# A two-layer graph network on one core: where the block C22 of an adding outer product is formed, with a new order of steps and new places beside it

## The chip, the core and the metric

The kernel runs on one core of a Trainium2 chip. The metric is the device time of one execution in microseconds (us); the figure quoted for a kernel is the median of several executions. The engines are called by the profile's short names: PE is TensorE (PEld its weight loads), DVE is VectorE, ACT is ScalarE, POOL is GpSimd, and SP is the engine whose queue issues nearly all DMAs. Each engine works its own queue in order and waits on semaphores where another engine's result is needed.

## The reference, cut to what matters

There are 128 graphs of 128 nodes with 512 features, all in fp32. Two layers follow one another, each with a residual and a layer norm:

```python
# layer 0
agg = einsum('bij,bjf->bif', adj, x) / max(sum(adj, -1), 1e-6)
x = layernorm(x + relu(concat([x, agg], 2) @ W.T))
# layer 1
Xw = x @ Wv + bv;  sj = Xw @ aw[:512];  si = Xw @ aw[512:]
a = adj * exp(leaky_relu(sj[:, None, :] + si[:, :, None] + ab, 0.2))
T = a / (sum(a, -1) + 1e-12)
H = x@Wk[0] + bk[0] + (T@x)@Wk[1] + bk[1] + (T@T@x)@Wk[2] + bk[2]
out = layernorm(x + relu(H))
```

## The kernel before, in words

**Groups and layers.** The graphs are worked in NG = 32 groups of G = 4. Layer 0 of all groups comes first, then layer 1 of all groups; the x between them goes through DRAM. Both layers multiply each group's transposed x with a weight matrix, and both do it by a Strassen-like scheme of seven block products in two levels. The change concerns layer 1. There the weights are `wg[o]`, o = 1 to 7, the outer level; each outer product is again made of seven products of 128x128 by 128x385.

**One outer product (`outer`, L613).** It is a generator of seven steps, named below O3.1 to O3.7 for outer product 3. It owns a *lane* of four PSUM banks called X, Y, W, Z. The lane `bA` is lane 1 and serves O1, O5, O7 and the combine; `bB` is lane 0 and serves O2, O6, O4, O3. Step by step: 1, a product into X, and ACT copies X to Y (L624); 2, a product into Z, and ACT copies Z to the SBUF tile s5 (L630; O5 adds a bias on DVE instead, L628); 3, a product onto X, and DVE writes W = X + s5 (L633); 4, a product onto Y, and Y is evicted as block C11; 5, a product onto X, and `direct` writes block C22 = X + s5 to SBUF (DVE, L657 or L670); 6, a product onto W, and W is evicted; 7, a product onto X, and X is evicted late, that is at the end of the step. The lane is then passed on with its banks turned: the next product's X is this one's Y, its Y this one's Z, its W this one's X, its Z this one's W.

**Two kinds.** O1 and O5 are *copying* (L652): evictions are ACT copies (L654). O2, O6, O7, O4, O3 are *adding* (L660): their result is added onto a block tile that another outer product left (`src`), so evictions are DVE additions (L663). For C22 the function `early` (L665) has POOL add the source block onto s5 in SBUF at step 3 (L667), and `direct` at step 5 has DVE add X and that s5 (L670). O3 adds onto the tile r after `sum_r` (POOL, L700) has added s to it.

**The combine (`combine`, L786), c.1 to c.8.** It multiplies the transition matrix TT twice: `one(b)` for b = 0 to 3 is a product of 512 columns, two DVE additions to v1 (L802, L803) and an ACT copy of the row back into the bank (L804); `two(b)` accumulates TT times v1 on top and DVE adds the residual late (L376). The order is one 0, one 1, one 2, two 0, one 3, two 1, two 2, two 3.

**What sets the order.** PE's order is written out by hand as lists of steps: PT (L829) for the passage from layer 0 to layer 1, PG (L830) for group 0 of layer 1, PB (L833) for groups 1 to 30, PL (L836) for group 31 with both its own O and c steps and a second combine x.1 to x.8 at the end. In PB, `o3.7` and `c.k` belong to the group before. One PB cycle has 57 steps: 49 products and 8 combine steps. Everything else is hung beside the steps: `PLACES_B` (L912) gives, for each other operation, a position of two per step counted from the start of the group's cycle (114 positions in a cycle): an even position 2s is run after the body of step s and before its late evictions, an odd one after them. `PLACES_M` and `PLACES_L` (L922, L927) do the same for the last two groups, `PLACES_S` for the passage. So the order of the list and the positions fix each engine's queue.

**The operations beside the steps** that the text speaks of: `x_turn` (DVE transpose of a loaded x tile, L255), `x_inner`, `x_s1` to `x_s4` (POOL sums of left blocks), `sum_r`, `sum_c` (POOL), `t_scores` (four small ACT operations, a DVE transpose L728, a DMA), `t_load`, `t_exp` (ACT, L750, L752), `t_sums` (POOL multiply L757, DVE reduce L759, a small ACT operation L760, DVE reciprocal L762), `t_norm` (ACT, and a DMA to DRAM), `t_back`, `t_turn` (DVE, L784), and for the layer norm `ln_mean`, `ln_scales` (POOL), `ln_var` (ACT, L500), `ln_apply` (ACT, L513), `y_store`; `load_left`, `load_y`, `load_adj` are SP's loads. For the last group `t_scores` builds a diagonal dg on DVE (L724), `t_exp` multiplies it with ones on PE, and `t_norm` turns the result with four PE products by the identity, each copied back by ACT (L777).

Of the kernel before, what the change touches and what calls it, by code (L numbers as in the profile page):

```python
# [16 lines left out]
def kernel(  # L17
# [15 lines left out]
    P = 128  # L33
# [62 lines left out]

    def load_adj(n):
        g = n % NG
        adjs[n] = p1.tile([P, G, N], FP, name="ag")
        nc.sync.dma_start(adjs[n], adj[g * G : (g + 1) * G].rearrange("b i j -> i b j"))  # L100

# [193 lines left out]
    def part(t, b, w=FH):  # L295
        return t[:, b[0], b[1], :w]
# [316 lines left out]
    def outer(lane, g, o, evict_y, direct, bias=False, early=None):  # L613
        need(*[("wg_load", o, i) for i in range(4)])
        n = NG + g
        X, Y, W, Z = [t[:, :BW] for t in lane]

        def prod(dst, k, start=False):
            mm(dst, left_of(n, o)[:, LEFT[k]], wg[o][:, RIGHT[k]], start)
        s5 = halves()[:, :BW]  # L620
        if bias:
            L_.copy(X, beta[:, 0])
        prod(X, 1, not bias)
        L_.copy(Y, X)  # L624
# [8 lines left out]
        V.tensor_add(W, X, s5)  # L633
        if early:
            early(s5)
        yield
        prod(Y, 2)
        evict_y(BY, Y)
        yield
        prod(X, 7)  # L640
        direct(X, s5)
        yield
        prod(W, 3)
        evict_y(BWW, W)
        yield
        prod(X, 4)
        late.append((evict_y, BX, X))
        a, b, c, d = lane
        lane[:] = [b, d, a, c]
        yield  # L650
# [9 lines left out]
    def adding(lane, g, o, dst, src, made=None):  # L660
        def evict(b, t):
            need(*[(made, g, {BY: 4, BWW: 6, BX: 7}[b])] if made else [])
            V.tensor_add(part(dst, b, BW), t, part(src, b, BW))  # L663

        def early(s5):  # L665
            need(*[(made, g, 5)] if made else [])
            S_.tensor_add(s5, s5, part(src, BZ, BW))  # L667

        def direct(X, s5):
            V.tensor_add(part(dst, BZ, BW), X, s5)  # L670
        yield from outer(lane, g, o, evict, direct, early=early)

    def o1(lane, g):
# [41 lines left out]
    def t_scores(g):  # L715
        need(("O3", g, 7), ("sum_c", g, 0), ("sum_c", g, 1))
        si = small.tile([P, G], FP, name="si")
        for p, t in ((0, rs[NG + g]), (1, last22[g])):
            L_.copy(sj[:, 2 * p : 2 * p + 2], t[:, :, 1, 381])
            L_.activation(si[:, 2 * p : 2 * p + 2], t[:, :, 1, 382], AF.Identity, bias=cc)  # L720
        if g == NG - 1:
            dg = p1.tile([P, G, N], FP, name="dg", tag="sb")
            for b in range(G):
                V.tensor_scalar(dg[:, b], ident, sj[:, b : b + 1], None, ALU.mult)  # L724
            Ts[g] = dg, si
            return
        turned = small.tile([P, R], FP, name="turned")
        V.transpose(turned, sj)  # L728
        d = dram.tile([R, Q, R], FP, name="scd")
        nc.sync.dma_start(d.rearrange("b q r -> q b r"), turned)  # L730
        Ts[g] = d, si

    def t_load(g):
        need(("t_scores", g))
# [4 lines left out]
        Ts[g] = T, si  # L739

    def t_exp(g):
        need(("t_load", g) if g < NG - 1 else ("t_scores", g))
        T, si = Ts[g]
        if g == NG - 1:
            dg, T = T, p1.tile([P, G, N], FP, name="T", tag="aT")
            pt = lanes[0][0]
            mm(pt, ones[:].to_broadcast([P, P]), dg, True)
        for b in range(G):
            src = T[:, b] if g < NG - 1 else pt[:, b * N : (b + 1) * N]
            L_.activation(T[:, b], src, AF.Prelu, bias=si[:, b : b + 1], alpha=SLOPE)  # L750
        Ts[g] = T, si
        L_.activation(T, T, AF.Exp)  # L752

    def t_sums(g):
# [10 lines left out]
    def t_norm(g):  # L765
        need(("t_sums", g))
        T, rr = Ts[g]
        for b in range(G):
            L_.activation(T[:, b], T[:, b], AF.Copy, scale=rr[:, b : b + 1])
        if g < NG - 1:  # L770
            swap_out(NG + g, T)
            return
        TTs[g] = p1.tile([P, G, N], FP, name="TT")
        for b in range(G):
            pt = lanes[0][1 + b // 2]
            mm(pt[:, b % 2 * N : (b % 2 + 1) * N], T[:, b], ident, b % 2 == 0)
            L_.copy(TTs[g][:, b], pt[:, b % 2 * N : (b % 2 + 1) * N])  # L777

    def t_back(g):
        Ts[g] = swap_in(NG + g)  # L780
# [5 lines left out]
    def combine(lane, g):  # L786
# [9 lines left out]
        v1 = {}  # L796

        def one(b):
            need(("O4" if b > 1 else "O3", g, 7), ("sum_c", g, 0), ("sum_c", g, 1))
            mm(at_[b], TTs[g][:, b], row(b, 0, F, 0), True)  # L800
            v = v1[b] = v1s[(g * G + b) % 3]
# [22 lines left out]
    def step(lane, name, g, k):  # L824
# [5 lines left out]
    PG = ("O5.1 O5.2 O5.3 O5.4 O2.5 O2.6 O6.1 O6.2 O5.5 O5.6 O5.7 O7.1 O6.3 O6.4 O7.2 "  # L830
          "O6.5 O2.7 O7.3 O6.6 O7.4 O6.7 O4.1 O4.2 O7.5 O4.3 O7.6 O7.7 O4.4 c.1 O4.5 "
          "O4.6 c.2 c.3 c.4 O4.7 O3.1 O3.2 O3.3 O3.4 c.5 c.6 c.7 c.8 O3.5 O3.6").split()
    PB = ("O1.1 o3.7 O1.2 O1.3 O2.1 O2.2 O1.4 O1.5 O1.6 O1.7 O2.3 O2.4 O5.1 O5.2 O5.3 O2.5 O2.6 O5.4 O5.5 "  # L833
          "O2.7 O6.1 O5.6 O6.2 O5.7 O7.1 O6.3 O7.2 O6.4 O6.5 O7.3 O6.6 O6.7 O7.4 O4.1 O4.2 O7.5 O4.3 O7.6 "
          "O4.4 O7.7 O4.5 c.1 c.2 O4.6 O4.7 O3.1 O3.2 c.3 c.4 O3.3 c.5 O3.4 c.6 c.7 c.8 O3.5 O3.6").split()
    PL = ("o3.7 O1.1 O1.2 O2.1 O1.3 O2.2 O1.4 O1.5 O1.6 O1.7 O2.3 O2.4 O5.1 O2.5 O2.6 O5.2 O2.7 O5.3 O5.4 O6.1 O5.5 O5.6 "  # L836
          "O6.2 O5.7 O6.3 O7.1 O6.4 O6.5 O7.2 O7.3 O7.4 O6.6 O7.5 O6.7 O7.6 O7.7 O3.1 O3.2 O3.3 O3.4 c.1 c.2 c.3 c.4 "
          "O3.5 c.5 c.6 c.7 c.8 O4.1 O3.6 O4.2 O3.7 O4.3 O4.4 O4.5 O4.6 O4.7 x.1 x.2 x.3 x.4 x.5 x.6 x.7 x.8").split()
    for s in PF:
        step(2 + "ABCD".index(s[0]), "F" + s[0], 0, int(s[2]))  # L840
    base = {}
# [39 lines left out]
    def place_op(n, pos, name, m, *a):  # L881
# [3 lines left out]
        else:  # L885
# [24 lines left out]
        ("load_adj", 1): 37, ("y_store", 0, 0): 161, ("ln_apply", 0, 0): 138, ("load_left", 2, 0): 78,  # L910
    }
    PLACES_B = {  # L912
        ("y_store", 0, 1): 281, ("sum_r", 0, 0): 80, ("sum_r", 0, 1): 84, ("sum_c", 0, 0): 115, ("ln_var", 0, 1): 229,
        ("x_inner", 1, 1): 34, ("load_y", 0, 0): 172, ("ln_var", 0, 3): 233, ("x_turn", 1, 0, 1): 29, ("t_turn", 0): 188,
        ("t_back", 0): 163, ("ln_var", 0, 2): 225, ("ln_mean", 0): 224, ("ln_apply", 0, 0): 245, ("x_s1", 1): 64,
        ("load_left", 2, 0): 83, ("y_store", 0, 0): 262, ("ln_apply", 0, 2): 274, ("load_left", 2, 1): 59,
        ("t_load", 0): 118, ("ln_var", 0, 0): 230, ("ln_apply", 0, 3): 255, ("x_turn", 1, 0, 0): 12, ("ln_scales", 0): 244,
        ("t_scores", 0): 117, ("t_norm", 0): 151, ("t_exp", 0): 139, ("load_y", 0, 1): 173, ("ln_apply", 0, 1): 255,
        ("x_s2", 1): 68, ("x_s4", 0): 49, ("x_turn", 1, 1, 0): 1, ("sum_c", 0, 1): 100, ("t_sums", 0): 150, ("x_s3", 1): 96,
        ("load_adj", 0): 116, ("x_inner", 1, 0): 36, ("x_turn", 1, 1, 1): 16,  # L920
    }
    PLACES_M = {  # L922
        ("ln_mean",): 213, ("ln_var", 1): 224, ("ln_scales",): 226, ("ln_var", 2): 222, ("ln_apply", 0): 234,
        ("ln_apply", 3): 237, ("ln_apply", 1): 230, ("y_store", 1): 255, ("ln_var", 0): 224, ("y_store", 0): 243,
        ("ln_var", 3): 213, ("ln_apply", 2): 242,
    }
    PLACES_L = {  # L927
        ("end_store", 2): 150, ("t_norm",): 115, ("sum_r", 0): 71, ("end_store", 0): 153, ("t_scores",): 105,
        ("sum_r", 1): 71, ("t_exp",): 107, ("end_apply", 0): 147, ("load_adj",): 96, ("end_apply", 1): 152,
        ("load_y", 1): 94, ("end_store", 1): 163, ("t_sums",): 111, ("end_stats", 3): 137, ("end_mean", 0): 125,  # L930
        ("end_apply", 2): 139, ("end_var", 1): 131, ("end_mean", 1): 130, ("end_stats", 2): 130, ("end_rstd", 2): 132,
        ("load_y", 0): 57, ("end_store", 3): 155, ("end_apply", 3): 151, ("end_scales",): 133, ("end_var", 0): 125,
        ("sum_c", 0): 76, ("end_rstd", 3): 145, ("sum_c", 1): 76,
    }
# [117 lines left out]
```

## Time and profile before

| what | value |
|---|---|
| median of three executions | 2092.91 us (2092.64 to 2092.97) |
| the profiled execution's own time | 2093.66 us |
| its span, first to last instruction | 2091.9 us |
| PE busy | 2074.7 us of the span |
| DVE, ACT, POOL busy | 1465.5, 1153.7, 1532.2 us |
| granted PE clock | 0.998 |
| layer 0 / passage and group 0 / groups 1 to 30 / rest | about 28 to 808 / 808 to 850 / 850 to 2027 / 2027 to 2092 us |

A row of a profile gives the engine, the line of the code, what is written and read by the program's names, how often, the time it was busy and the mean of one, and after the bar the idle time of the engine just before it with what ended that. In a timeline a row begins with its start and its duration in us, and the bracket at the end tells how long the engine stood idle before it and for whom. A fp32 product stands in the trace as two matmul records and two weight loads.

### The profile page before, as it was taken

How to read it: one execution, taken by the hardware profiler on the slowest of the kernel's cores; microseconds unless marked ns; L12 is line 12 of the kernel's file. 1: busy time of each engine (PE TensorE's matmuls, PEld its weight loads, DVE VectorE, ACT ScalarE, POOL GpSimd, SP SyncE). 2: the span in 40 equal slices, each digit the busy share in tenths (PEclk: the TensorE clock that was granted, in tenths of full speed). 3: DMA queues.
4: the chain of work that ended last, by engine and by line, in shares of the span. 5: the costliest groups of instructions: out<-in, count | busy, mean ns of one | idle time of the engine just before them, and what ended most of it. 6: DMA issues, size and time to landing. Idle time of an engine off the chain costs nothing.

```text
span 2091.9 us, 25884 instructions
## 1 busy us (share of the span) xinstructions
PE 2074.7 (99%) x7100; PEld 1330.3 (64%) x7100; DVE 1465.5 (70%) x3247; ACT 1153.7 (55%) x2883; POOL 1532.2 (73%) x1424
## 2 busy tenths in 40 slices
PE   9999999999999999999999999999999999999997
PEld 6778888888778886555555555555555555555553
DVE  6777777777777777666666666666666666666665
ACT  2656666666666666355455455455455455455454
POOL 5777888887767776867767767767767767767763
PEclk9999999999999999999999999999999999999999
DMA  9777766676667767335534434534534534534523
GB/s 207 171 189 194 180 178 178 161 190 194 158 165 190 188 171 237 87 86 122 115 87 122 115 86 122 115 86 122 115 86 124 114 86 124 113 87 122 115 66 116
DMA packets 429486, 287.13 MB, mean 137 GB/s; under 512 B 153497, under 2 KB 352281, under 8 KB 429340
## 3 DMA queue, kind: packets, MB, share of 16 engines
q1 hardware_dynamic: 428412, 284.15, 53.7%
q10 hardware_dynamic: 800, 1.31, 0.3%
q8 instruction: 56, 0.92, 0.2%
q14 instruction: 90, 0.74, 0.1%
q0 software_dynamic: 128, 0.01, 0.0%
HBM read 191.60 MB, written 93.79 MB: 136 GB/s over the span
## 4 chain that ended last, share of the span: by engine, by line
PE 96%; DMA 1%; POOL 1%; DVE 1%; ACT 0%; issue 0%; ACTq 0%; DVEq 0%; POOLq 0%
PE bA L151 50%; PE bB L151 45%; DMA big<-in_w0t_dram 1%; DMA yd<-y 0%; DMA xb<-in_x_dram 0%; DMA y<-in_x_dram 0%; PE bA L177 0%; POOL s L667 0%; POOL c L711 0%; POOL r L703 0%; ACT junk L500 0%; DVE y L376 0%; POOL xs L266 0%; POOL xs L270 0%; POOL xu L278 0%
## 5 line engine op out<-in xcount | busy, mean ns | idle before, releaser
L151 PE MATMUL bB<-big,xu 128*128 128x385 f32 (+1 forms) x1806 | 562.1, 434 | 0.7 <-DVE r L670 0.5
L151 PEld LDWEIGHTS bB<-big,xu 128*128 128x128 f32 x1806 | 341.8, 190 | 167.7 <-issue 44.8
L151 PE MATMUL bA<-big,xl 128*128 128x256 f32 (+1 forms) x1358 | 405.8, 416 | 0.4 <-DVE bA L471 0.3
L151 PE MATMUL bB<-big,xs 128*128 128x256 f32 (+1 forms) x1316 | 384.1, 416 | 0.0
L151 PEld LDWEIGHTS bA<-big,xl 128*128 128x128 f32 x1358 | 257.1, 190 | 100.1 <-issue 15.6
L151 PEld LDWEIGHTS bB<-big,xs 128*128 128x128 f32 x1316 | 249.1, 190 | 84.8 <-ACT bB L624 6.2
L151 PE MATMUL bA<-big,xu 128*128 128x256 f32 (+1 forms) x896 | 294.3, 440 | 0.4 <-DVE bA L633 0.2
L667 POOL TENSOR_TENSOR s<-s,r 128x385 f32<-128x385 f32 x128 | 128.1, 1001 | 182.2 <-DVE bB L633 139.1
L151 PE MATMUL bA<-c,TT 128*128 128x512 f32 x512 | 241.3, 593 | 0.0
L500 ACT ACTIVATE junk<-y,mv 128x512 bf16<-128x512 f32 x252 | 182.6, 725 | 89.5 <-POOL mv L495 85.3
L151 PEld LDWEIGHTS bA<-big,xu 128*128 128x128 f32 x896 | 162.0, 189 | 95.4 <-DVE r L657 19.3
L513 ACT ACTIVATE y<-y,mv,rstd 128x512 f32<-128x512 f32 x252 | 202.1, 815 | 0.6 <-POOL mv L508 0.6
L376 DVE SCALAR_TENSOR_TENSOR y<-bA,y 128x512 f32<-128x512 f32 x256 | 170.5, 684 | 23.4 <-PE bA L151 16.9
L151 PE MATMUL bA<-big,xs 128*128 128x385 f32 x448 | 173.7, 499 | 0.0
L151 PE MATMUL bB<-big,xl 128*128 128x385 f32 (+1 forms) x462 | 172.0, 480 | 0.8 <-ACT bA L452 0.4
L633 DVE TENSOR_TENSOR bB<-bB,s 128x385 f32<-128x385 f32 x128 | 72.5, 567 | 121.0 <-PE bB L151 83.2
L151 PEld LDWEIGHTS bA<-c,TT 128*128 128x128 f32 x512 | 97.2, 190 | 89.4 <-issue 48.8
L624 ACT COPY bB<-bB 128x385 f32<-128x385 f32 x128 | 60.1, 470 | 143.8 <-PE bB L151 143.8
L278 POOL TENSOR_TENSOR xu<-xu,xs 128x896 f32<-128x896 f32 x63 | 131.7, 2090 | 8.8 <-PE bB L151 8.8
L274 POOL TENSOR_TENSOR xl<-xu,xl 128x896 f32<-128x896 f32 x63 | 133.5, 2120 | 1.1
L270 POOL TENSOR_TENSOR xs<-xs,xu 128x896 f32<-128x896 f32 x63 | 132.0, 2095 | 2.4
L266 POOL TENSOR_TENSOR xs<-xl 128x896 f32<-128x896 f32 x63 | 131.3, 2085 | 0.0
(182 smaller groups left out, 3474.8 us busy)
## 6 DMA issues: line engine op xcount, KB each, us to landing
xb<-in_x_dram SPq DMA_DIRECT2D x256, 128.0 KB, 3.8
y<-in_x_dram SPq DMA_DIRECT2D x64, 512.0 KB, 4.2
yd<-y SPq DMA_DIRECT2D x64, 512.0 KB, 3.0
xb<-yd SPq DMA_DIRECT2D x256, 128.0 KB, 5.2
y<-yd SPq DMA_DIRECT2D x64, 512.0 KB, 4.6
out_dram<-y SPq DMA_DIRECT2D x62, 512.0 KB, 2.8
ag<-in_adj_dram SPq DMA_DIRECT2D x64, 256.0 KB, 5.1
sb<-sd SPq DMA_DIRECT2D x252, 64.0 KB, 3.2
```

The lines of the kernel that those rows point to most:

```text
L151: nc.tensor.matmul(dst, lhsT, rhs, start=start, stop=True, skip_group_check=True)
L266: S_.tensor_add(xs[n][:, 0], xl[n][:, 0], xl[n][:, 1])
L270: S_.tensor_sub(xs[n][:, 1], xs[n][:, 0], xu[n][:, 0])
L274: S_.tensor_sub(xl[n][:, 0], xu[n][:, 0], xl[n][:, 0])
L278: S_.tensor_sub(xu[n][:, 1], xu[n][:, 1], xs[n][:, 1])
L376: V.scalar_tensor_tensor(y, t, 0.0, y, ALU.max, ALU.add, accum_out=mvs[n][:, b, 0:1])
L500: L_.activation(junk, ys[n, b // 2][:, b % 2], AF.Square, bias=mvs[n][:, b, 0:1], accum_out=mvs[n][:, b, 1:2])
L513: L_.activation(y, y, AF.Identity, bias=mvs[n][:, b, 0:1], scale=rstds[n][:, b : b + 1])
L624: L_.copy(Y, X)
L633: V.tensor_add(W, X, s5)
L667: S_.tensor_add(s5, s5, part(src, BZ, BW))
```

## The change

In `adding`, the source block of C22 is no longer added onto s5 by POOL. DVE writes Z + source into the destination block, from the PSUM bank Z of step 2, and at step 5 adds X onto that destination block. For O6, O7, O4 and O3 this stands in step 3 behind W = X + s5; for O2 it stands in step 4 behind the eviction of Y. The lists PB and PL and the tables PLACES_B, PLACES_M and PLACES_L are replaced; PT, PG, PLACES_S and PLACES_A stay.

For the last group alone the transition matrix is made in another way. Its adjacency is loaded by blocks and turned by DVE (`adj_turn`). dg is built from si instead of sj; after the product with ones, ACT applies Prelu with bias sj and Exp pair by pair, so that the matrix comes out turned (`end_scores`). `end_rows` multiplies by the turned adjacency on DVE (two halves of 256 columns) and has PE sum over partitions by a product with ones; `end_norm` adds the epsilon, takes the reciprocal of 256 columns and multiplies, all on DVE. The four PE turns by the identity, their ACT copies, and `t_exp`, `t_sums`, `t_norm` are not run for that group.

Among the places moved in the PB cycle: `x_turn` (1,1,0) from position 1 to -5, which is step 54 of the cycle before; the other two-part turns to steps 7 and 9; `load_left` (2,1) from 59 to 70; `t_sums` to 149, in front of the late eviction of O2.7; `sum_r` (0,1) to 81 and (0,0) to 86; `load_adj` from 116 to 103, `y_store` (0,1) to 278, in front of `t_back` at 165.

```diff
@@ load_adj
+        if n == 2 * NG - 1:
+            adjs[n] = p1.tile([P, G, Q, R], FP, name="agb", tag="ag")
+            load_blocks(adjs[n], adj[g * G : (g + 1) * G])
+            return
@@ outer
         V.tensor_add(W, X, s5)
-        if early:
-            early(s5)
+        if early and o != 2:
+            early(Z)
         yield
         prod(Y, 2)
         evict_y(BY, Y)
+        if early and o == 2:
+            early(Z)
@@ adding
-        def early(s5):
+        def early(Z):
             need(*[(made, g, 5)] if made else [])
-            S_.tensor_add(s5, s5, part(src, BZ, BW))
+            V.tensor_add(part(dst, BZ, BW), Z, part(src, BZ, BW))

         def direct(X, s5):
-            V.tensor_add(part(dst, BZ, BW), X, s5)
+            V.tensor_add(part(dst, BZ, BW), X, part(dst, BZ, BW))
@@ new for the last group
+    def adj_turn():
+        need(("load_adj", 2 * NG - 1))
+        src = adjs[2 * NG - 1]
+        adjs[2 * NG - 1] = p1.tile([P, G, N], FP, name="agT", tag="aT")
+        V.transpose(adjs[2 * NG - 1].rearrange("p g n -> p (g n)"), src.rearrange("p g j r -> p (g j r)"))
+    def end_scores(g):
+        need(("t_scores", g), ("C", g - 1, 8))
+        (dg, _), pt = Ts[g], lanes[0][0]
+        mm(pt, ones[:].to_broadcast([P, P]), dg, True)
+        T = TTs[g] = p1.tile([P, G, N], FP, name="TT")
+        for b in range(G):
+            L_.activation(T[:, b], pt[:, b * N : (b + 1) * N], AF.Prelu, bias=sj[:, b : b + 1], alpha=SLOPE)
+            if b % 2:
+                L_.activation(T[:, b - 1 : b + 1], T[:, b - 1 : b + 1], AF.Exp)
+    def end_rows(g, h):
+        need(("end_scores", g), ("adj_turn",))
+        T = TTs[g][:, 2 * h : 2 * h + 2].rearrange("p b n -> p (b n)")
+        pt = lanes[0][1 + h][:, :FH]
+        V.tensor_mul(T, T, adjs[2 * NG - 1][:, 2 * h : 2 * h + 2].rearrange("p b n -> p (b n)"))
+        mm(pt, ones[:].to_broadcast([P, P]), T, True)
+    def end_norm(g, h):
+        need(("end_rows", g, h))
+        T = TTs[g][:, 2 * h : 2 * h + 2].rearrange("p b n -> p (b n)")
+        pt = lanes[0][1 + h][:, :FH]
+        rr = halves()[:, :FH]
+        V.tensor_scalar(rr, pt, ROW_EPS, None, ALU.add)
+        V.reciprocal(rr, rr)
+        V.tensor_mul(T, T, rr)
@@ order of steps, new lists
+    PB = ("O1.1 o3.7 O1.2 O1.3 O2.1 O1.4 O1.5 O1.6 O2.2 O1.7 O2.3 O2.4 O5.1 O5.2 O2.5 O5.3 O2.6 O5.4 O2.7 "
+          "O6.1 O5.5 O6.2 O5.6 O6.3 O5.7 O6.4 O7.1 O6.5 O6.6 O7.2 O7.3 O6.7 O4.1 O7.4 O7.5 O4.2 O4.3 O7.6 "
+          "O4.4 O4.5 O7.7 c.1 O4.6 O4.7 O3.1 O3.2 c.2 O3.3 c.3 c.4 c.5 c.6 c.7 c.8 O3.4 O3.5 O3.6").split()
+    PL = ("O1.1 o3.7 O1.2 O2.1 O1.3 O2.2 O1.4 O1.5 O1.6 O1.7 O2.3 O2.4 O5.1 O2.5 O5.2 O2.6 O2.7 O5.3 O5.4 O6.1 O5.5 O6.2 "
+          "O5.6 O5.7 O6.3 O7.1 O6.4 O6.5 O7.2 O7.3 O6.6 O7.4 O7.5 O6.7 O7.6 O7.7 O3.1 O3.2 O3.3 O3.4 c.1 c.2 c.3 c.4 "
+          "c.5 c.6 c.7 c.8 O4.1 O3.5 O4.2 O3.6 O3.7 O4.3 O4.4 O4.5 O4.6 O4.7 x.1 x.2 x.3 x.4 x.5 x.6 x.7 x.8").split()
@@ PLACES_B, new
+        ("t_norm", 0): 154, ("sum_r", 0, 1): 81, ("load_y", 0, 0): 170, ("ln_var", 0, 3): 230, ("x_turn", 1, 0, 1): 19,
+        ("t_back", 0): 165, ("x_s1", 1): 66, ("ln_scales", 0): 239, ("t_sums", 0): 149, ("x_turn", 1, 1, 1): 19,
+        ("load_left", 2, 0): 82, ("ln_var", 0, 1): 227, ("y_store", 0, 0): 264, ("t_turn", 0): 187, ("ln_var", 0, 2): 224,
+        ("sum_c", 0, 0): 109, ("ln_apply", 0, 2): 273, ("ln_apply", 0, 3): 257, ("x_inner", 1, 1): 53, ("ln_var", 0, 0): 235,
+        ("t_exp", 0): 140, ("load_left", 2, 1): 70, ("ln_apply", 0, 1): 257, ("y_store", 0, 1): 278, ("x_s2", 1): 68,
+        ("x_turn", 1, 1, 0): -5, ("x_s3", 1): 97, ("ln_apply", 0, 0): 242, ("t_load", 0): 123, ("t_scores", 0): 119,
+        ("x_turn", 1, 0, 0): 14, ("sum_r", 0, 0): 86, ("x_s4", 0): 42, ("load_adj", 0): 103, ("load_y", 0, 1): 190,
+        ("ln_mean", 0): 223, ("sum_c", 0, 1): 115, ("x_inner", 1, 0): 41,
@@ PLACES_L, new
...
+        ("end_store", 2): 158, ("sum_c", 1): 72, ("sum_r", 0): 71, ("end_store", 0): 158, ("t_scores",): 105,
+        ("end_var", 1): 134, ("sum_r", 1): 71, ("load_adj",): 96, ("load_y", 0): 47, ("end_apply", 1): 160,
+        ("load_y", 1): 106, ("end_mean", 1): 128, ("end_rows", 0): 111, ("end_mean", 0): 127, ("end_rstd", 2): 132,
...
+        ("sum_c", 0): 76, ("end_rstd", 3): 149, ("end_apply", 0): 144, ("end_scores",): 106, ("end_rows", 1): 111,
+        ("end_norm", 0): 111, ("end_stats", 3): 138, ("end_norm", 1): 111, ("end_apply", 3): 158, ("adj_turn",): 96,
```

## The prediction, made before the changed kernel was run

> **What bounds the kernel now.** I read first the busy shares, then busy time by stretch (us from the start; PE, PEld, DVE, ACT, POOL), then the weight loads' timeline in one steady cycle, then who held the weight loads between 860 and 2050, then DVE's timeline in group 0 and PE's at the end.
>
> ```profile
> PE 2074.7 (99%) x7100; PEld 1330.3 (64%) x7100; DVE 1465.5 (70%) x3247; ACT 1153.7 (55%) x2883; POOL 1532.2 (73%) x1424
> ```
> ```profile
> 850.50:2026.60 1176.10, 1175.49 (x3416) 636.96 (x3417) 778.14 (x1619) 607.58 (x1488) 863.77 (x777) 1.00 0.44 107
> 2064.00:2091.90 27.90, 15.50 (x38) 6.82 (x36) 13.15 (x34) 15.42 (x39) 6.76 (x14) 0.85 0.20 75
> ```
> PE is the bound, and idle only at the end. But a record lasts until its drain: a 385-column record is shown as 487 ns, while two in a row start 323 ns apart (512 columns: 429). So waits of up to 0.16 us lie inside "busy", and I read starts. A PB cycle holds 98 records of 385 and 16 of 512 columns: 98 x 0.323 + 16 x 0.429 = 38.52 us. Measured from cycle to cycle: 39.22. So 0.70 us per cycle is lost, 30 x 0.70 = 21 us in all; more than that this change cannot win there.
>
> ```profile
> 1012.65 0.19 PEld L151 LDWEIGHTS bA<-big,xu 128*128 128x128 f32 x1
> 1013.46 0.30 PEld L151 LDWEIGHTS bA<-big,xu 128*128 128x128 f32 x2 [0.62 <-DVE r L657]
> 1013.90 1.16 PEld L151 LDWEIGHTS bB<-big,xu 128*128 128x128 f32 x4
> 1015.56 0.94 PEld L151 LDWEIGHTS bA<-big,xs 128*128 128x128 f32 x4 [0.51 <-issue]
> 1017.03 0.30 PEld L151 LDWEIGHTS bA<-big,xs 128*128 128x128 f32 x2 [0.53 <-ACT bA L624]
> ```
> ```profile
> PEld bA L151 <- DVE r L657: 18.6, 30, 0.6
> PEld bA L151 <- ACT bA L624: 15.7, 30, 0.5
> PEld bA L151 <- DVE bA L633: 11.8, 30, 0.4
> ```
> Thirty of each: one per cycle (the time is that of PEld's idling, its usual rest included; what PE loses is less). By starts, O1.7 loses 0.27 us (O1.5 stands only two steps ahead and `direct` isn't done), O5.3 0.18 (the copy Y = X of O5.1, two steps ahead), O5.1 0.16 (ACT reaches the beta copy L622 late), O1.5 0.05 (its W). Sum 0.65; the rest is jitter. **None of the four waits for POOL**: `early` on POOL is hidden in the steady cycle. It costs only in group 0:
>
> ```profile
> 843.64 0.56 DVE L670 TENSOR_TENSOR c<-bB,s 128x385 f32<-128x385 f32 x1 [0.41 <-POOL s L667]
> 850.18 0.56 DVE L670 TENSOR_TENSOR r<-bB,s 128x385 f32<-128x385 f32 x1 [1.52 <-POOL s L667]
> ```
> ```profile
> 2066.00 1.12 PE L151 MATMUL bB<-dg,ones 128*128 128x512 f32 x2 [0.79 <-DVE dg L724]
> 2066.97 3.09 PE L151 MATMUL bA<-big,xl 128*128 128x385 f32 x8
> 2072.29 0.49 PE L151 MATMUL bB<-ident,T 128*128 128x128 f32 x2 [2.23 <-ACT T L769]
> 2073.32 1.14 PE L151 MATMUL bB<-ident,T 128*128 128x128 f32 x4 [0.54 <-ACT TT L777]
> ```
> The last fence is the end: PE waits for the last transition matrix, and the last combine starts at 2075.41.
>
> **The Trainium skill.** "Perfetto Trace Analysis", Identifying the Most-Contended Engine, says that matmul busy share is no measure because matmuls are pipelined: agrees (0.70 us per cycle hidden at 99%). "TensorE: Matmul & The Clock Gate", Specifications: PE pulls weight loads ahead of running matmuls. Agrees: undisturbed, a load starts 2 ns after the matmul before it; a waiting one isn't pulled, and starts 0.053 after the release, with 0.107 more before its product runs. **So PE stalls unless the reader has ended 0.16 us before** (0.22 where it waits for two engines). "GPSIMD Engine Reference", Specifications: no PSUM access, which is why `early` needed s5; no run here tests it.
>
> **The change, part by part.** I walk a cycle from T = 0 at O1.1, a product 0.646, a combine step 0.858. A reader of a product's bank starts 0.847 after the step's start (1.058 for a combine step); DVE then takes 0.56 (385 columns; next one starts 0.46 later), a turn 0.70 (0.625), ACT 0.47 (0.36 to 0.41), all from rows and starts around 1007 to 1046.
>
> *`early` on DVE.* Five POOL additions of 1.00 go per cycle, five DVE ones come: 2.3 (by spacing) to 2.8 us. DVE rises from 25.96 to some 28.5 of 39.2, POOL falls from 28.84 to 23.8. Queued behind each are the eviction of step 4 and `direct`. The work that covers it: W is written ahead of it, and PE needs `direct` only at step 7, at least three steps after step 5 in the new list wherever an adding product is concerned: 1.94 against 0.847 + 0.56 + 0.16 = 1.57. Without that cover it would cost up to 0.46 per product, 2.3 per cycle. I take 0.
>
> *New order.* O2.2 now stands between O1.6 and O1.7, O2.5 between O5.2 and O5.3: three steps each, 1.94 against 1.57 and 1.48. **Those 0.27 + 0.18 = 0.45 go.** What is late next:
> - c.5 to c.8 now run without a product between. c.5's additions, row copy and release: 1.058 + 0.343 + 0.412 + 0.089 + 0.592 + 0.16 = 2.654 against 3 x 0.858 = 2.574: 0.08. Before, in the last group, the same four in a row lost 0.10.
> - `x_turn` (1,1,0), moved to step 54, stands in DVE's queue ahead of `direct` of O3.5 and the eviction of O3.6. c.8's residual frees DVE at 37.48, eviction 37.48, turn 37.96, `direct` 38.59 to 39.14, + 0.16 = 39.30; o3.7 is due at 38.52 + 0.65 = 39.16: 0.14.
> - O1.5: s5 of O1.2, then `t_scores` on ACT, its DVE turn (L728), then W: 2.66 after O1.2 against 2.58: 0.08.
> - O5.1: eviction of O1.6, then `ln_apply`, s5 of O2.2, eviction, beta: 3.39 against 3.23: 0.16 as before.
>
> Sum 0.46 for 0.65: **0.19 to 0.20 per cycle, 29 cycles, 5.7 us.** Each of the four is good to about 0.1 either way.
>
> *Other places.* `t_sums` now stands ahead of O2.7's eviction and `direct` of O5.5. The chain (T's load issued at 5.2 lands 3.2 later, median of its issues; Prelu 9.1, Exp to 11.1, POOL multiply to 12.4, reduce to 13.2, reciprocal 13.6) frees `direct` at 14.0; O5.7 needs it by 15.5: cost 0, margin 0.96. SP: `y_store` stands ahead of `t_back`, which waits for its own swap anyway (sd lands 2.3 after 15.1); `load_left` (2,1) has 19 steps, 12.3 us, for four issues of 0.5 and 5.2 of landing; `load_adj`, now at the cycle's end, finds its buffer freed by the multiply at 12.4: 0. POOL queue: `sum_r` (0,1) comes before (0,0) and ends near 29.5, before O3's `early` at 32.1. ACT: in the last group one `ln_var` now stands ahead of `t_scores`; it ends at 2065.3 on the old clock, before r's block is there at 2065.5: 0.
>
> *Passage and group 0* (order unchanged). O4.7 waited 0.59 for L670 behind POOL; now only the two-step distance, 0.33: -0.26. o3.7 waited 0.80: gone. `sum_c` then ends 0.9 + 0.9 us earlier on POOL (two `early` less ahead), so O1.5's 0.46 shrinks to 0.04. Against it DVE is jammed from 822 to 828 by late residuals, and O2's `early` adds 0.45. Sum -1.0; bounds -1.6 to 0.
>
> *Last group.* o3.7 loses its 0.34. O3's `early` waits on DVE for `sum_r` half 1, queued second on POOL (done at 2055.15 by the old times): the eviction, then c.1's additions come behind it and c.4 loses 1.0. So dg's product starts 1.2 later, 2067.2. Then Prelu and Exp of the first pair to 2069.5, multiply, rows; Exp of the second to 2070.5, multiply, rows at 2071.0; add 0.40, reciprocal, multiply. **The reciprocal of 256 columns is in no row.** Low: 0.42, as a multiply of 256. High: the skill's "VectorE: DVE Perf Modes", First, the fixed hardware budget, gives it a repeat count of 8: an estimate of (256 x 8 + 151)/0.96 = 2.3 us. Its row of 4 elements takes 178 ns against 161 for an addition of 4: 4 ns more an element, so some 5.3 x 256 + 157 = 1.5 us. I take 1.5. Then x.1 starts at 2073.6 instead of 2075.4, but the second half's norm and O4.6's eviction behind it hold x.3 for 1.1 and x.4 for 0.9, where before the waits in the combine came to 1.05: PE ends 0.7 earlier, with o3.7 1.1. Bounds: -3.2 with 0.42, +0.6 with 2.3. The chain of norms and stores after it keeps its length.
>
> **Sum.** -5.7 - 1.0 - 1.1 = -7.8. The profiled execution took 2093.66 (span 2091.9 and 1.8 around it): 2085.9. The median shown is 0.75 lower, 2092.91: **2085.0.**
>
> **Rivals.**
> - *Clean*: all of 0.65 goes and no new wait comes (my 0.16 rule too strict): 2092.9 - 29 x 0.65 - 2.1 = 2072. For it: three of the new stalls are within 0.14 of nothing. Against: O5.1's chain is not touched.
> - *Moved*: the waits only change place, 0.6 to 0.7 per cycle: 2092.9 - 2.1 = 2091. For it: four margins below 0.1 that sum against me if ACT or DVE runs 0.05 later.
> - *Slower*: DVE's head. `t_sums`' reduce waits for POOL and ACT with `direct` of O5.5 behind it. It decides once T's chain is over 0.96 us later than walked; each us beyond costs PE one in every cycle. Half a us: 29 x 0.5 - 7.8, +6.7: 2100. For it: this wait is new at that place. Against: POOL's multiply is first in its queue now.
> - *Not done as said*: excluded; the edit is plain.
>
> **Numbers.** Forecast (2080 to 2089 by itself) 0.60, clean 0.13, moved 0.17, slower 0.10. A measurement tells 0.2%, 4.2 us, from no change. Faster: forecast nearly whole, clean: 0.72; same: moved and a rest: 0.18; slower 0.10. Range 2073 to 2092: it leaves out slower (0.10) and the far half of clean (0.06), and holds the bounds of passage and end (-4.8 to +0.6 for -2.1) and four stalls each 0.1 off with the same sign (29 x 0.4 = 12, taken halfway).
>
> **What would show it.** Cycle 39.02 by starts (38.6 clean, over 39.2 moved); no wait of PE on L657 at O1.7, nor on L624 at O5.3; waits at o3.7, O1.5, O5.1, c.8 of the sizes above; no L667; a reciprocal row of 256 columns near 1.5 us; x.1 near 2066.6 (2075.4 - 1.8 - 0.3 - 5.7 - 1.0). Wrong if the weight loads wait 30 times on a step not named here.

## The result, and the profile after

| | before | after |
|---|---|---|
| median, us (lowest to highest, runs) | 2092.91 (2092.63 to 2093.38, 5) | 2084.6 (2083.08 to 2085.31, 5) |
| profiled execution, us (its span) | 2093.66 (2091.9) | 2083.08 (2081.3) |
| one steady cycle by starts, us | 39.220 | 38.912 |
| start of the last group to the start of PE's last record, us | 55.41 | 55.61 |

The ratio is 0.9958, with an interval of 0.9948 to 0.9969: 8.3 us less. The profiled execution of the changed kernel is the fastest of its five, that of before lies 0.75 above its median, so the two traces differ by 10.6.

The busy shares first. VectorE rises by 60 us and POOL falls by 155, while PE stays at 99%:

```profile
PE 2062.5 (99%) x7096; PEld 1329.9 (64%) x7096; DVE 1525.8 (73%) x3414; ACT 1155.7 (56%) x2875; POOL 1377.7 (66%) x1263
```

Who held the weight loads between 855 and 2040 (waited-for line: us in total, times, longest):

```profile
PEld bA L155 <- ACT bA L831: 19.3, 31, 0.7
PEld bB L155 <- DVE r L676: 13.7, 29, 0.8
PEld bA L155 <- DVE bA L637: 9.2, 29, 0.3
PEld bA L155 <- DVE r L663: 0.6, 1, 0.6
```

The wait of O1.7 for `direct` (L663 here, L657 before) has fallen from 30 to one, in the last group, whose own list still has O1.7 two steps behind O1.5 (it loses 0.27 us there); the wait of O5.3 for the copy Y = X is gone. New are 29 waits for L676, the `direct` of O3 (o3.7), and for L831, the row copy of a combine (c.8). The same stretch of one cycle as a timeline of weight loads (start, us, engine, line, what; in brackets the idle time and its cause):

```profile
1083.16 0.30 PEld L155 LDWEIGHTS bB<-big,xu 128*128 128x128 f32 x2 [0.46 <-DVE r L676]
...
1086.37 0.97 PEld L155 LDWEIGHTS bA<-big,xu 128*128 128x128 f32 x4 [0.32 <-DVE bA L637]
...
1088.77 1.16 PEld L155 LDWEIGHTS bB<-big,xu 128*128 128x128 f32 x4
1090.44 0.94 PEld L155 LDWEIGHTS bA<-big,xs 128*128 128x128 f32 x4 [0.51 <-issue]
```

These are o3.7, O1.5, the run of loads from O2.2 over O1.7 to O2.3, now without a wait, and O5.1. Idle time of PEld is not PE's loss; by starts of the matmuls PE loses per cycle 0.113 us at o3.7, 0.161 at O5.1, 0.075 at c.8 and nothing at O1.5, whose load waits but is done in time. Sum 0.35, where before it was 0.65 (O1.7 0.270, O5.3 0.176, O5.1 0.156, O1.5 0.051).

The last group on PE and on VectorE:

```profile
2046.53 1.13 PE L155 MATMUL bA<-big,TT 128*128 128x512 f32 x2 [0.80 <-ACT bA L831]
...
2055.83 1.12 PE L155 MATMUL bB<-dg,ones 128*128 128x512 f32 x2 [0.78 <-DVE dg L730]
...
2062.70 1.13 PE L155 MATMUL bA<-c,TT 128*128 128x512 f32 x2 [1.04 <-DVE TT L770]
2065.74 1.98 PE L155 MATMUL bA<-c,TT 128*128 128x512 f32 x4 [1.92 <-DVE c L669]
```
```profile
2044.11 0.56 DVE L673 TENSOR_TENSOR r<-bB,r 128x385 f32<-128x385 f32 x1 [0.94 <-POOL r L709]
...
2060.43 1.75 DVE L769 RECIPROCAL s<-s 128x256 f32<-128x256 f32 x1
...
2063.01 1.75 DVE L769 RECIPROCAL s<-s 128x256 f32<-128x256 f32 x1
...
2065.14 1.02 DVE L669 TENSOR_TENSOR c<-bA,c 128x385 f32<-128x385 f32 x2
```

c.4 stalls behind `early` of O3, which waits on VectorE for POOL's second sum; the reciprocal takes 1.75 us; x.1 starts 6.87 us after dg's product (9.40 before), but x.2 then stalls for 2.19 us: its bank is the W of O4, and O4.6's eviction of it stands on VectorE behind the second half's norm (it ends at 2065.69; x.2 starts at 2065.74).

Span by stretches, after against before: the start and the first layer, which the change leaves alone, 0.9 less; passage and group 0, 1.3 less; 29 cycles 8.9 less (the first 0.24 of o3.7's old wait in the last group is counted here); the last group 0.2 more, with 0.28 more behind PE's last record. Sum -10.6.

### The profile page after: what moved, and what is told of

It is laid out like the page before. It is cut to its first block, busy times and chain, and to the rows that moved or that the text cites. A ratio compares the mean times of both kernels' runs of the same rounds, so it can differ in the third digit from the quotient of the medians.

```text
span 2081.3 us, 25875 instructions
## 1 busy us (share of the span) xinstructions
PE 2062.5 (99%) x7096; PEld 1329.9 (64%) x7096; DVE 1525.8 (73%) x3414; ACT 1155.7 (56%) x2875; POOL 1377.7 (66%) x1263
## 4 chain that ended last, share of the span: by engine, by line
PE 97%; DVE 1%; DMA 1%; ACT 0%; issue 0%; POOL 0%; SPq 0%; ACTq 0%; DVEq 0%
PE bA L155 51%; PE bB L155 46%; DMA yd<-y 0%; DMA xb<-in_x_dram 0%; DMA y<-in_x_dram 0%; PE bA L181 0%; DVE s L769 0%; DVE y L380 0%; POOL r L709 0%; ACT y L517 0%; DVE big L995 0%; DVE xl L259 0%; DVE xu L259 0%; DVE big L1003 0%; SPq L83 0%
## 5 line engine op out<-in xcount | busy, mean ns | idle before, releaser
L155 PE MATMUL bB<-big,xu 128*128 128x385 f32 (+1 forms) x1806 | 569.5, 435 | 1.0 <-DVE c L676 0.7
L155 PE MATMUL bA<-big,xl 128*128 128x256 f32 (+1 forms) x1358 | 395.9, 416 | 0.3 <-DVE bA L475 0.3
L155 PE MATMUL bB<-big,xs 128*128 128x256 f32 (+1 forms) x1316 | 388.8, 416 | 0.0
L155 PEld LDWEIGHTS bA<-big,xl 128*128 128x128 f32 x1358 | 256.8, 189 | 100.1 <-issue 15.5
L155 PE MATMUL bA<-c,TT 128*128 128x512 f32 x512 | 245.9, 592 | 3.0 <-DVE c L669 1.9
L380 DVE SCALAR_TENSOR_TENSOR y<-bA,y 128x512 f32<-128x512 f32 x256 | 170.4, 683 | 19.6 <-PE bA L155 13.4
L155 PE MATMUL bA<-big,xs 128*128 128x385 f32 x448 | 178.3, 492 | 0.0
L709 POOL TENSOR_TENSOR r<-r,s 128x770 f32<-128x770 f32 x64 | 115.1, 1820 | 86.4 <-DVE c L669 86.4
L155 PE MATMUL bB<-big,xl 128*128 128x385 f32 (+1 forms) x462 | 167.2, 480 | 0.5 <-ACT bA L456 0.4
L790 POOL TENSOR_TENSOR T<-ag,T 128x512 f32<-128x512 f32 x31 | 39.5, 1275 | 175.9 <-ACT T L785 175.9
L499 POOL TENSOR_SCALAR mv<-mv 128x4 f32<-128x4 f32 x63 | 14.5, 230 | 212.3 <-DVE y L380 212.3
L831 ACT COPY bA<-r 128x512 f32<-128x512 f32 x64 | 37.7, 590 | 176.4 <-DVE big L830 170.7
L637 DVE TENSOR_TENSOR bB<-bB,s 128x385 f32<-128x385 f32 x128 | 72.5, 567 | 85.1 <-PE bB L155 75.4
```

The costliest lines, as they stand in the source:

```text
L155: nc.tensor.matmul(dst, lhsT, rhs, start=start, stop=True, skip_group_check=True)
L380: V.scalar_tensor_tensor(y, t, 0.0, y, ALU.max, ALU.add, accum_out=mvs[n][:, b, 0:1])
L499: S_.tensor_scalar(mvs[n][:, :, 0], mvs[n][:, :, 0], -1.0 / F, None, ALU.mult)
L709: S_.tensor_add(r, r, s)
L790: S_.tensor_mul(T, adjs[NG + g], T)
L831: L_.copy(at_[b], row(b, 254, 766, 1))
```

## The experiments

Each kernel was run beside the kernel before on the same chip; the last columns are the difference of the two medians and the steady cycle in its trace. The changed kernel stands at -8.3 in this table.

| kernel | us | before there | difference | cycle |
|---|---|---|---|---|
| 1 move alone | 2092.63 | 2092.77 | -0.1 | 39.204 |
| 2 all but the move | 2095.20 | 2092.77 | +2.4 | 39.286 |
| 3 turn later | 2081.32 | 2092.77 | -11.5 | 38.851 |
| 4 `ln_apply` later | 2079.38 | 2092.77 | -13.4 | 38.751 |
| 5 O3.4 between | 2099.45 | 2093.28 | +6.2 | 39.416 |
| 6 sums exchanged | 2085.92 | 2093.28 | -7.4 | 38.912 |
| 7 old last group | 2086.30 | 2093.28 | -7.0 | 38.912 |
| 8 exponentials later | 2096.44 | 2093.28 | +3.2 | 39.300 |
| 9 addition twice | 2098.24 | 2093.84 | +4.4 | 39.297 |
| 10 three waits mended | 2075.61 | 2093.84 | -18.2 | 38.641 |
| 11 and O3.4 between | 2086.47 | 2093.84 | -7.4 | 39.022 |

The theory: the gain is the order of steps, which takes two waits off PE; `early` on VectorE is hidden. The rival: POOL was the brake, and taking work off it gains. No run takes the new list and the new places apart for O1.7 and O5.3. That the list frees them is read from the traces: with three steps instead of two in between they lose nothing, and O1.7 of the last group, still at two, loses its 0.27.

**1. The move alone**, in the kernel before (the calls of `early` are changed with it, and O2's stands in step 4, as in the change):

```diff
-            S_.tensor_add(s5, s5, part(src, BZ, BW))
+            V.tensor_add(part(dst, BZ, BW), Z, part(src, BZ, BW))
...
-            V.tensor_add(part(dst, BZ, BW), X, s5)
+            V.tensor_add(part(dst, BZ, BW), X, part(dst, BZ, BW))
```

> The kernel before with only the fifth product's addition moved to VectorE; step order, places and end as before. Theory (the order is the gain, the move by itself is hidden): the four waits of a steady cycle (O1.7, O5.3, O5.1, O1.5) wait for nothing on POOL, so the cycle stays at 39.22 us; group 0 and the passage gain about 1.3, the last group loses about 0.6 because O3's addition now holds VectorE until POOL has summed half 1 of r: 2092.2 us. Rival (the move off POOL is what gains): the whole change of about 8 us is here, cycle 38.9, 2084.5 us.

Ratio 0.9998 (0.999 to 1.0007): nothing. The four waits stand as before (O1.7 0.269, O5.3 0.175, O5.1 0.154, O1.5 0.040). Passage and group 0 give 1.15 back, and in the last group c.4 loses 1.06. The rival "POOL was the brake" falls for the old order.

**2. All but the move**: the changed kernel with the four lines of 1 turned round (O2's addition, on POOL again, stays in step 4).

> The changed kernel with the fifth product's addition back on POOL; order, places and new end kept. Plain form of the theory (order alone): cycle stays 38.91, passage +1.3, last group -1.0, 2085 us. Refined form, from POOL's queue walked with the five additions put back: O4's stands behind the two x sums that start at 64.9 and 67.0 and now 1.3 later, ends near 71.4 where O4.5's last addition started at 70.5, so O4.7 loses 0.26 per cycle: cycle 39.17, near 2092 us; then order and move gain only together. Rival (the move is the gain): all 8 us are gone for lack of POOL, with waits on POOL at several steps, not at O4.7 alone, 2093 or more.

Ratio 1.0011 (1.0004 to 1.0017), cycle 39.286. The plain form of the theory, order alone, falls too. The refined form named the cause; its size was short. POOL, VectorE and the weight loads in one cycle:

```profile
1068.39 2.09 POOL L270 TENSOR_TENSOR xs<-xl 128x896 f32<-128x896 f32 x1
1070.56 2.09 POOL L274 TENSOR_TENSOR xs<-xs,xu 128x896 f32<-128x896 f32 x1
1072.59 1.01 POOL L673 TENSOR_TENSOR s<-s,c 128x385 f32<-128x385 f32 x1
```
```profile
1073.63 0.56 DVE L676 TENSOR_TENSOR c<-bB,s 128x385 f32<-128x385 f32 x1 [1.11 <-POOL s L673]
```
```profile
1074.24 0.30 PEld L155 LDWEIGHTS bB<-big,xl 128*128 128x128 f32 x2 [0.43 <-DVE c L676]
...
1075.84 0.30 PEld L155 LDWEIGHTS bB<-big,xu 128*128 128x128 f32 x2 [0.65 <-DVE c L669]
```

O4's addition comes behind two sums of 2.09 us each on POOL, `direct` of O4.5 waits for it with VectorE idle for 1.11 us, and behind `direct` stand the evictions: O4.7 loses 0.07 (0.26 expected) and O3.2, which the expectation did not name, 0.30. O1.7 and O5.3 stay free. So order and move gain only together: the new order takes the waits away, and needs VectorE to do the addition, because the places of POOL's work in it leave none in time. Whether other places for POOL's sums would let the order gain without the move, no run tried.

**3. The turn later**:

```diff
-        ("x_turn", 1, 1, 0): -5,
+        ("x_turn", 1, 1, 0): 1,
```

> The changed kernel with x_turn (1,1,0) back at place 1, behind O3.6's eviction. Theory: o3.7's wait of 0.112 us per cycle is that turn ahead of the last addition of O3, and VectorE has 0.9 us free between O3.6's and o3.7's evictions, so the cycle falls to 38.80: 29 x 0.112 = 3.2 us, 2081.4 us. Rival (VectorE's five new additions make the wait, the turn only happens to stand there): cycle stays 38.91, 2084.6 us.

Ratio 0.9948 (0.9936 to 0.9961). o3.7's wait is gone, as the list of holders shows by what it lacks (no L676 29 times); that of L637, O1.5's W, has grown from 9.2:

```profile
PEld bA L155 <- ACT bA L831: 19.4, 31, 0.7
PEld bA L155 <- DVE bA L637: 11.6, 29, 0.4
```

Half of the gain in the cycle comes back at O1.5: 0.113 goes, 0.052 comes, 38.851 instead of 38.80. That the time, 2081.32, meets the expected 2081.4 is therefore luck: the steady cycles give 29 x 0.061 = 1.8 us and a longer cycle that is missing here (see the end) 0.35, not 3.2. In its trace ACT's copy of the scores of C22 starts 0.03 us after the end of `sum_c`, which POOL does behind `ln_mean`.

**4. `ln_apply` later**:

```diff
-        ("ln_apply", 0, 0): 242,
+        ("ln_apply", 0, 0): 256,
```

> The changed kernel with ln_apply (0,0) moved from 242 to 256, behind the exponentials of the transition matrix. Theory: O5.1's 0.161 us per cycle is ACT's queue, where this 0.81 us operation stands ahead of three copies that O5.1 waits for; without it the copy of beta ends near 51.25 on the clock of the cycle at 1043.25, 0.07 before it is due: cycle 38.75, 29 x 0.161 = 4.7 us, 2079.9 us. Rival: O5.1 waits for O1.7's bank, 2.5 steps ahead, whatever ACT does: cycle 38.91. Third: ACT, with three such operations in a row behind the exponentials, makes the row sums late: O5.7 loses, slower.

Ratio 0.9936 (0.9924 to 0.9949). O5.1 loses nothing any more, the cycle is 38.751: 0.161 less, to the nanosecond what the stall was.

**5. O3.4 between c.5 and c.6**:

```diff
-          "... c.2 O3.3 c.3 c.4 c.5 c.6 c.7 c.8 O3.4 O3.5 O3.6"
+          "... c.2 O3.3 c.3 c.4 c.5 O3.4 c.6 c.7 c.8 O3.5 O3.6"
```

> The changed kernel with step O3.4 between c.5 and c.6 instead of behind c.8. Theory: c.8's 0.074 us is the distance of three combine steps from c.5 to c.8; with a product between, it has 0.57 to spare. VectorE then also reaches the turn ahead of O3.5's last addition without O3.4's eviction before it, so o3.7's 0.112 goes too: cycle 38.73 (38.84 if only c.8's goes), 29 x 0.186 = 5.4 us, 2079.2 us (2082.4). Rival (VectorE, now 28.5 us busy per cycle, is late there whatever the order): the wait reappears at another step between c.5 and O1.2 and the cycle stays above 38.88.

Ratio 1.0028 (1.0018 to 1.0039), cycle 39.416: both forms of the theory fall. c.8's stall is gone; o3.7 loses 0.188 and O1.5 0.478. c.8 comes one step later, and with it its residual, for which `ln_mean` waits; behind `ln_mean` POOL does `sum_c`, and behind that ACT takes the scores:

```profile
1045.12 0.23 POOL L499 TENSOR_SCALAR mv<-mv 128x4 f32<-128x4 f32 x1 [4.81 <-DVE y L380]
1045.32 3.59 POOL L717 TENSOR_TENSOR c<-c,s 128x770 f32<-128x770 f32 x2
```
```profile
1048.94 0.19 ACT L725 COPY sj<-c 128x2 f32<-128x2 f32 x1
```

POOL lay idle for 4.81 us and then did 3.59 us of sums, whose inputs had long been there; the copy starts at 1048.94, as they end. The short turn and W of O1.5 follow it.

**6. The two sums of the last group exchanged**:

```diff
-        ("sum_r", 0): 71, ..., ("sum_r", 1): 71,
+        ("sum_r", 1): 71, ("sum_r", 0): 71,
```

> The changed kernel with the two halves of sum_r in the last group exchanged, half 1 first on POOL. Theory: c.4's stall of 1.07 us in the last group is O3's fifth-product addition waiting on VectorE for half 1, so it goes and nothing else changes: last group 1.0 shorter, 2083.5 us. The transition matrix isn't touched by it: dg's product still waits 1.05, the combine's third step 2.2. Rival (the end is bound by VectorE's norm chain, so a stall ahead of it is slack): the end keeps its length and the stall at dg's product grows by 1.

Ratio 0.9963 (0.9951 to 0.9976); c.4 loses 1.24 instead of 1.07. Now `early`, which needs half 1, passes, and the eviction behind it, which needs half 0, waits:

```profile
2042.91 0.55 DVE L673 TENSOR_TENSOR r<-bB,r 128x385 f32<-128x385 f32 x1
2044.57 0.56 DVE L669 TENSOR_TENSOR r<-bB,r 128x385 f32<-128x385 f32 x1 [1.11 <-POOL r L709]
```

With `early` on VectorE the two instructions stand side by side and need both halves at once; neither order of the sums helps. The theory of the stall was half of it.

**7. The old last group** with the rest of the change; its order, its places and its way to the transition matrix are those of before:

```diff
-    PL = ("O1.1 o3.7 O1.2 O2.1 O1.3 O2.2 O1.4 O1.5 O1.6 O1.7 O2.3 O2.4 O5.1 O2.5 O5.2 O2.6 O2.7 O5.3 O5.4 O6.1 O5.5 O6.2 "
+    PL = ("o3.7 O1.1 O1.2 O2.1 O1.3 O2.2 O1.4 O1.5 O1.6 O1.7 O2.3 O2.4 O5.1 O2.5 O2.6 O5.2 O2.7 O5.3 O5.4 O6.1 O5.5 O5.6 "
...
```

> The change without its new last group: order and places of the steady cycle and the additions on VectorE as in the changed kernel, last group and its transition matrix as before. As predicted (the new end is worth 1.1 in all, 0.7 after dg's product): 2085.7 us. From the traces so far: between dg's product and the last matmul the new end takes 16.2 us at full clock, the old one 16.9 of which some 1.4 is PE at half clock; so at equal clock the new end is 0.7 longer: 2083.9 us, and in both kernels the part at half clock differs from run to run by up to 3 us.

Ratio 0.9965 (0.9953 to 0.9978), which overlaps that of the changed kernel and holds both expected forms: whether the new last group gains can't be told from the times. The traces show why the comparison is loose. PE's granted clock near the end differs from run to run; here two kernels with the same last combine, first experiment 2, then the changed kernel (busy time by stretch; the number after POOL's is the clock):

```profile
2076.00:2082.00 6.00, 5.42 (x7) 2.33 (x8) 3.16 (x9) 2.69 (x5) 0.00 (x0) 0.50 0.00 0
```
```profile
2066.00:2072.00 6.00, 5.90 (x13) 2.15 (x13) 4.91 (x14) 4.82 (x8) 0.45 (x2) 1.00 0.13 52
```

At 0.50 two records of 512 columns start 0.853 us apart instead of 0.429. Added up by starts, this cost the profiled run of before 1.4 us, of the changed kernel nothing, of experiment 7 2.9. Without it, from dg's product to the start of the last record: before 15.5, experiment 1 15.4, experiment 7 15.8; the new end 15.7 to 16.2 in the other traces. So at equal clock the new end is no shorter there, as far as this sum can tell: no trace has the old end at full clock throughout.

**8. The exponentials later**, the rival "slower" of the prediction:

```diff
-        ("t_exp", 0): 140,
+        ("t_exp", 0): 144,
```

> The changed kernel with the exponentials of the transition matrix (t_exp) at 144, behind two ln_apply on ACT, so that the matrix comes about 1.6 us later. It prices the predicted slower rival: the reduce stands on VectorE ahead of O2.7's eviction and O5.5's last addition, which in the changed kernel end 1.0 before O5.7 is due. Theory: O5.7 loses 1.6 - 1.0 = 0.6 to 0.7 us per cycle, 19 us, 2103.5 us. Rival (VectorE's wait is absorbed elsewhere, the margin is larger than walked): 2084.6 us.

Ratio 1.0015 (1.0008 to 1.0022), cycle 39.300: 0.388 more. The matrix came 1.40 us later (the reduce starts 13.98 us into a steady cycle, 12.58 in the changed kernel), not 1.6, and 1.40 less the margin of 1.0 is about the 0.39 lost. It is lost in two places, 0.29 at O6.3, where ACT's copy Y = X stands behind the row sums, and 0.10 at O5.7 for `direct`:

```profile
PEld bB L155 <- ACT bB L628: 18.6, 29, 0.7
...
PEld bA L155 <- DVE s L663: 12.9, 29, 0.4
```

**9. The addition twice**, to try VectorE's cover:

```diff
+            V.tensor_add(halves()[:, :BW], Z, part(src, BZ, BW))
             V.tensor_add(part(dst, BZ, BW), Z, part(src, BZ, BW))
```

> The changed kernel with each fifth-product addition done twice on VectorE, the first time into a buffer that nobody reads: five more additions of 0.55 us per cycle, 2.3 us by spacing. Theory (the move is hidden behind VectorE's idle time): four of the five fit where they stand; O3's pushes the additions behind it, so that c.4's residual ends 0.3 late for c.5's additions and c.8 loses 0.38 instead of 0.074: cycle 39.2, 29 x 0.3 = 8.9 us, 2093.5 us. Rival (VectorE is the second bound and every addition on it costs its spacing): 2.3 x 29 = 67 us, 2151 us. Third (all hidden): 2084.6 us.

Ratio 1.0021 (1.0012 to 1.003), cycle 39.297: 0.385 more for 2.3 us of added work. c.8 loses 0.354 as expected (0.28 more); O3.2 loses 0.103, which was not expected, as VectorE's stretch from O4.4 to c.1 has less room than a second addition:

```profile
PEld bA L155 <- ACT bA L832: 42.4, 60, 0.9
...
PEld bB L155 <- DVE c L669: 13.6, 30, 0.5
```

VectorE isn't the second bound: five sixths of the work put on it cost nothing.

**10. Three waits mended**, with experiments 3 and 4, both `sum_c` ahead of `ln_mean`, and O3's `early` in the last group behind c.8:

```diff
+        ... ("x_turn", 1, 1, 0): 1, ... ("ln_apply", 0, 0): 256, ...
+        ("sum_c", 0, 0): 100, ... ("sum_c", 0, 1): 101, ...
...
-        if early and o != 2:
+        if early and o != 2 and (o, g) != (3, NG - 1):
             early(Z)
         ...
         prod(X, 7)
+        if early and (o, g) == (3, NG - 1):
+            early(Z)
         direct(X, s5)
```

> The changed kernel with its step order kept, x_turn (1,1,0) at 1, ln_apply (0,0) at 256, both sum_c placed ahead of ln_mean on POOL (100 and 101), and in the last group O3's fifth-product addition moved behind c.8, into step O3.5. Theory: o3.7's 0.112 and O5.1's 0.161 go together; the 0.052 at O1.5 that the later turn alone had brought was ACT's copy waiting for sum_c behind ln_mean on POOL, so it stays away; c.4's stall of 1.07 in the last group goes: cycle 38.64, 2084.6 - 29 x 0.273 - 1.0 = 2075.7 us. Rival (ACT or VectorE bounds O1.5, not POOL): O1.5 loses 0.05 again, cycle 38.69, 2077.2 us. For the end, rival (what bounds it is VectorE's later norm chain): c.4's stall goes, and dg's product comes no earlier.

2075.61 us, ratio 0.9914 (0.99 to 0.9928), cycle 38.641. Only c.8's 0.075 is left of the steady stalls, and O1.5's wait is back at the 9.2 that cost nothing:

```profile
PEld bA L155 <- ACT bA L833: 20.0, 32, 0.7
PEld bA L155 <- DVE bA L637: 9.2, 29, 0.3
```

So the 0.052 of experiment 3 was POOL's queue; `ln_apply`, which moved too, stands behind O1.5's copies in ACT's queue. In the last group c.4's stall of 1.07 is gone but for the 0.07 that it had before the change, O3.7 now loses 0.20, and dg's product comes 38.37 us after the group's start instead of 39.40. Of these 1.03 us 0.8 is thus the moved addition, and 0.23 is a wait of O5.1 that went with `ln_apply`: the rival for the end falls, though the stall did not come back whole.

**11. And O3.4 between c.5 and c.6**:

```diff
-          "... c.5 c.6 c.7 c.8 O3.4 O3.5 O3.6"
+          "... c.5 O3.4 c.6 c.7 c.8 O3.5 O3.6"
```

> The kernel before this one in the list with O3.4 between c.5 and c.6 as well. Theory: O3.4 there cost 0.48 at O1.5 because c.8, and so its residual, ln_mean and both sum_c behind it on POOL, came one step later, and 0.19 at o3.7 because the turn stood ahead of O3.5's last addition; with both out of the way only its gain is left, c.8's 0.074: cycle 38.57, 2073.5 us. Rival (with O3.5 and O3.6 straight behind c.8 the residuals themselves make VectorE late, whatever POOL and the turn do): o3.7 or O1.5 still lose 0.1 to 0.4, slower than the one before, 2078 us or more.

2086.47 us, ratio 0.9965 (0.9953 to 0.9978), cycle 39.022. c.8 and o3.7 lose nothing; O1.3 loses 0.213 and O1.5 0.245:

```profile
PEld bA L155 <- DVE bA L637: 17.4, 30, 0.6
PEld bA L155 <- ACT bA L628: 16.3, 29, 0.6
```

```profile
1083.43 0.72 ACT L504 ACTIVATE junk<-y,mv 128x512 bf16<-128x512 f32 x1 [2.84 <-POOL mv L499]
...
1084.99 0.47 ACT L628 COPY bA<-bA 128x385 f32<-128x385 f32 x1
```

The rival's sizes came, but not its cause: it had the residuals make VectorE late. POOL is out of the way, but the same late `ln_mean` also releases four `ln_var` of 0.9 us each on ACT. They start 0.65 us later in the cycle than in experiment 10, so that O1.1's copy Y = X, which stands behind two of them, ends 2.00 us into the cycle instead of 1.35, and O1.2's s5, behind a third, at 3.11 instead of 2.62. c.8's place is held by what follows from its residual, on two engines; its 0.075 us can't be had by moving O3.4 alone.

## Why the prediction was right, point by point

The forecast was 2085.0 us, the time 2084.6. Its mechanism held, and two of its terms were off with opposite signs. That the total came within 0.4 us is in part luck: added up by stretches in the two traces, the change saved 9.7 us where the forecast had 7.8.

- **The order takes 0.45 per cycle.** Held: O1.7 lost 0.270 and O5.3 0.176 before, nothing after. But the reason that it gains was stated as the order's alone, with the move "at nothing". Experiments 1 and 2 show that neither gains by itself; the walk of VectorE's cover was right, and what the move spares in the new order, POOL's late O4 addition, was not walked at all.
- **What is late next.** c.8 0.08, measured 0.075; o3.7 0.14, measured 0.113; O5.1 0.16, measured 0.161. Experiments 3 and 4 removed the last two by the cause named, and 10 both together. The rule "0.16 us before the product is due" held for all of them.
- **O1.5 0.08: measured 0.** The mis-sized term of the steady sum. I had W start when the short turn of the scores is done, 0.21 by its row; it starts 0.136 after the turn's start (1046.870 against 1046.734), so W ends 2.40 after O1.2, not 2.50, and with 0.16 is in time for 2.58. So the saving is 0.31 per cycle, not 0.20, and 29 cycles give 8.9 instead of 5.7.
- **`early` on VectorE at nothing.** Held in the steady cycle: in experiment 2, with the addition on POOL, o3.7, O5.1 and c.8 lost the same 0.113, 0.158 and 0.076. Experiment 9 put a second one behind each and lost 0.385, so the margin is less than 0.46 at O3 and O4 and enough elsewhere.
- **Passage and group 0, -1.0.** Measured -1.3: o3.7 lost 0.04 (0.80 before), O1.5 0.16 (0.46), O4.7 0.27 (0.59), O2.7 0.96 (0.30; I had +0.45, it is +0.66). These four give -0.7; about -0.4 more is the steady gain of group 1's own cycle, which lies in this stretch and which the forecast did not count, so that the sum agrees better than its terms. Experiment 1 alone has -1.15 there.
- **The last group, -1.1: measured 0.0 with o3.7's wait, and 0.28 more behind it.** The step that failed. Its front part held: c.4 1.07 (1.0), x.1 1.6 earlier counted from the group's first product, 1.9 with o3.7's wait (1.8 and o3.7's 0.3). The reciprocal took 1.75 us (1.5). The forecast had O4.6's eviction hold x.3 for 1.1 and x.4 for 0.9; it holds x.2, for 2.19, and x.4 loses 0.37. x.2 writes the bank that O4.6 leaves, and it is due one combine step, 0.86, before x.3; with the second reciprocal 0.25 longer than walked, 1.1 + 0.86 + 0.25 = 2.21. Both norms and the eviction lie on VectorE without a gap from 2059.97 to 2065.69. (The expectation of experiment 6 names the combine's third step as well.) And the 1.05 us of "waits in the combine" that I took off before's end were in the main no waits: PE ran at half clock there (records 0.853 apart at 2075.41), which is a matter of the run and not of the kernel.
- **Clean, moved and slower** did not come. The margin that the slower rival needed, 0.96, was 1.0 in experiment 8, and the chain would have to be that much later than it is.

So the total was right with 3.2 us too little in the cycles and 1.4 too much at the end; the first layer's 0.9 and the 1.5 by which the profiled run is faster than its median belong to no step.

## What to carry to other kernels

A gain from reordering belongs to the order and to whatever lets its queues keep up: try each half by itself before giving the credit to one. When a step is moved, follow what its last reader releases on every engine, not only the engines named in the step; here c.8, moved by one step, made `ln_mean` late, and through it POOL's sums and ACT's squares, and each looked free by itself. An operation that waits for long and is short belongs behind work that is ready: two sums placed ahead of `ln_mean` on POOL, with the turn and `ln_apply` moved off the path and O3's addition in the last group put behind c.8, took another 9.9 us; the sums' own part is about 29 x 0.052 = 1.5 us, an estimate from experiments 3 and 10.

## What the runs showed of the hardware

- **The reciprocal of 128 x 256 takes 1.753 us**, four times the 0.42 of a multiply of the same shape. "VectorE: DVE Perf Modes", First, the fixed hardware budget, speaks of a repeat count of 8, from which I had estimated 2.3 us; with the same fixed part the measured row is 6.0 cycles a column, and the measurement decides.
- **PE's clock halves in the last group**, in nine of the eleven traces of the experiments and in that of before, each time within or shortly after a stretch in which PE lay idle for 1.9 to 2.6 us, and for 3.41 or 6.83 us while PE still had work (2073.43 to 2076.84 in the trace of before). "TensorE: Matmul & The Clock Gate", Part 1: The HAM clock gate, has half rate after an idle window of about 3.4 us and full rate after as long a busy one. The half rate agrees (0.50, 0.853 us against 0.429), and so does the length of the phases, one or two such windows; the idle stretches here were shorter than one. The changed kernel, experiment 5 and experiment 10 had the same idle stretches and no such phase of note, and no run here tells what decides.
- **One cycle is 0.35 us longer** in the traces of the changed kernel and of experiments 4 and 6 to 8, at o3.7 of group 5 each time, and in that of experiment 9 at o3.7 of group 19. All have the turn at -5 and the sums behind `ln_mean`, but so have experiments 2 and 5, which lack it. There the eviction of O3.4 on VectorE starts only as `ln_mean` on POOL ends. With the turn at 1 (experiments 3, 10 and 11) it isn't there. Why it comes once, stays open.
